# A fixed order of work in layers 1 to 3, dense and listed tiles mixed, and smaller table rows in layer 0, in a four-layer graph attention kernel

## The chip, the cores and the metric

The kernel runs on one core of one Trainium2 chip. The metric is the device time of one execution in microseconds; lower is better. Before the change it is 4248.78 us, the median of three runs (4247.72, 4248.78 and 4255.99).

## The reference: what is computed

There are 4096 nodes with 256 features and a 0/1 adjacency matrix of 4096 x 4096 whose density falls from the first node to the last, so the first rows have many neighbours and most rows few. Four attention layers follow one another, each as `x = layernorm(x + layer(x, adj))`:

```python
# layer 0, 8 heads: a neighbour j of i weighs
#   exp(leaky_relu(e_l[i] + e_r[j], 0.2) + gate * sum_f |c[i,f] - c[j,f]| * Wc[h,f])
# layer 1, one head: weight exp(s_src[i] + s_dst[j])
# layer 2, 4 heads: exp(leaky_relu(s_row[i] + s_col[j], 0.2)); elu(out) + x @ Wr + br, then a layernorm of its own
# layer 3, one head, three times: h = x @ W0, then h = elu(softmax(mask(leaky_relu(f1 + f2.T, 0.01))) @ (h @ W))
```

Each weight is masked by the adjacency and divided by its row's sum. A row without any neighbour takes the mean over all nodes instead, which the kernel carries as `cs`.

## The kernel before, in words

**Lists.** For each block of columns of the result (128 destination rows in layer 0, 256 in the later layers, called a pair, `PW`) the kernel finds the nodes with at least one edge into it. From the adjacency it makes bytes on ScalarE (`ab`, L669), counts edges per node on TensorE (`flags`, L676), ranks them (`places`) and builds each list by comparing ranks with a counter on VectorE (`here`, L715, four instructions a list) and 32 small matmuls on TensorE (`list_p`, L729). A list has a fixed number of tiles of 128 nodes: `SLOT_TILES` for layer 0 (373 in all) and `PAIR_TILES` for the pairs (251 without the first). For a listed pair the mask is gathered too, one tile at a time (`pair_m`, L742, and `pair_mb`, L746), and stored in DRAM.

**Layer 0** first projects x (class `Projection`, `rows`), scales the result and writes it into `table0`, one row of 368 numbers per node: 264 weighted features, 8 factors, and the node's 6 curvature numbers repeated 16 times (96). Then `rows0` walks over the 373 tiles, in blocks of 3 or 4 tiles (107 blocks). A tile's table rows `g` and adjacency cells `m` are gathered by indirect DMAs on GpSimd (L419, L421). Per block TensorE transposes the curvature part of each `g` (`cj_p`, L431), ScalarE copies it and makes 8 differences `d` (L438). Per tile TensorE computes the scores `s` (2 x L453, 16 x L457), ScalarE takes `e = exp(s)` (L459), VectorE multiplies in the row factors (8 x L475), and TensorE adds the products to `acc` (16 x L481), two tiles later. This loop stands under `tc.manual_schedule`: TensorE, VectorE and ScalarE run their instructions in the order in which the program writes them. In each tile's round the program writes: `edges` (the mask `ne` of the next tile, L445), `pair_terms` (scores and `e`), `weights`, the `add` of two tiles before, one third of the next block's `differences` (`parts`), one step of a row end (`end`), and `lane(n + 1)`. The lane takes 1.5 steps a tile from one generator, `all_groups`, in which flags and lists of the later groups follow one another, and one job (`step`): a piece of a mask.

**Layers 1 to 3.** `layer1`, `layer2` and `layer3` loop over pairs (`plan_of`: two dense pairs, then listed pairs with the other dense pairs between), and within a pair over its tiles. A dense pair has 32 tiles, all nodes, whose rows lie in SBUF; a listed pair's rows are gathered from a table in DRAM (`Nodes.rows`, L908). Per tile VectorE (in layer 1 `nc.any`, ScalarE or VectorE) makes the weights `w` (L983, L1048, L1121), and TensorE multiplies (L991; L1050 for the sums and L1053 for the denominators; L1123). After a pair's last tile the program writes its whole row end: `quotients`, the residual and layernorm, and the projection for the next layer (`project_rows`; `Projection.steps`, with `xT` L182, `ph` L186, `V` L189, `f2` L190, and for layers 2 and 3 a separate product `pf` L197 for the second score vector, which goes through DRAM). These layers have no order written out by hand: the compiler's own scheduler places the instructions of each engine by priority and readiness in its model. `DENSE` gives the number of dense pairs: 6 in layer 1, one in layer 2, 3 in each pass of layer 3.

Of the kernel before, what the change touches and what calls it, by code (L numbers as in the profile page):

```python
# [49 lines left out]
F32 = mybir.dt.float32  # L50
# [19 lines left out]
DENSE = {1: 6, 2: 1, 3: 3}  # L70


@with_exitstack
def gnn_stack(ctx: ExitStack, tc: tile.TileContext, a: dict, out: bass.AP):
# [36 lines left out]


    class Projection:
# [6 lines left out]

        def __init__(self, name, nh, scores, nf, w, wt, V=None, f1=None, bias=None, pre=None, extra=None,
                     done=None):
            self.name, self.nh, self.nf, self.V, self.f1, self.bias, self.extra = name, nh, nf, V, f1, bias, extra
            self.w, self.wt, self.scores, self.pre, self.done = w, wt, scores, pre, done
            self.f2 = carry.tile([P, NT, nh], F32, name=f"{name}_f2", tag="f2")
            self.xs = carry.tile([P, 2, NT], F32, name=f"{name}_xs", tag="xs")
            self.cs = carry.tile([P, nh, C // nh + 1], F32, name=f"{name}_cs", tag="cs")

        def prepare(self, st, ps):

            self.ps = ps
            nh, nf = self.nh, self.nf
            wp = st.enter_context(tc.tile_pool(name=f"{self.name}_w", bufs=1))
            self.xp = st.enter_context(tc.tile_pool(name=f"{self.name}_x", bufs=2))
            wx = wp.tile([P, 2, C + nf], F32, name="wx")
            nc.gpsimd.dma_start(wx[:, :, 0:C], self.w.rearrange("(k p) o -> p k o", p=P))
            wt = wp.tile([P, 2, C], F32, name="wt")
            nc.gpsimd.dma_start(wt, self.wt.rearrange("(k p) o -> p k o", p=P))
            amat = wp.tile([P, 2, nf], F32, name="amat")
            nc.vector.memset(amat, 0.0)  # L140
            for kt, p0, n, col, vec in self.scores:
                nc.gpsimd.dma_start(amat[p0:p0 + n, kt, col:col + 1], vec)
            for mt in range(2):
                pw = ps([P, nf], "pw")
                for kt in range(2):
                    nc.tensor.matmul(pw, wt[:, kt, mt * P:(mt + 1) * P], amat[:, kt, :], start=kt == 0, stop=kt == 1)
                nc.vector.tensor_copy(wx[:, mt, C:], pw)
            if self.pre is not None:
                pre = wp.tile([P, 2, C], F32, name="pre")
                nc.gpsimd.dma_start(pre, self.pre.rearrange("(k p) o -> p k o", p=P))  # L150
                both = wp.tile([P, 2, C + nf], F32, name="both")
                for mt in range(2):
                    pw = ps([P, C + nf], "pw")
                    for kt in range(2):
                        nc.tensor.matmul(pw, pre[:, kt, mt * P:(mt + 1) * P], wx[:, kt, :], start=kt == 0, stop=kt == 1)
                    nc.vector.tensor_copy(both[:, mt, :], pw)
                wx = both
            self.wx = wx
            if self.bias is not None:
                self.bx = wp.tile([P, C + nh], F32, name="bx")  # L160
                nc.gpsimd.dma_start(self.bx[:, 0:C], self.bias.partition_broadcast(P))
                bcol = wp.tile([P, 2, 1], F32, name="bcol")
                nc.gpsimd.dma_start(bcol, self.bias.rearrange("(k p o) -> p k o", p=P, o=1))
                wide = wp.tile([P, 2, P], F32, name="bwide")
                nc.vector.tensor_copy(wide, bcol.to_broadcast([P, 2, P]))
                pb = ps([P, nf], "pb")
                for kt in range(2):
                    nc.tensor.matmul(pb, wide[:, kt, :], amat[:, kt, :], start=kt == 0, stop=kt == 1)
                nc.vector.tensor_copy(self.bx[:, C:], pb[:, 0:nh])
            if self.extra is not None:  # L170
                self.wr = wp.tile([P, 2, C], F32, name="wr")
                nc.gpsimd.dma_start(self.wr, self.extra[0].rearrange("(k p) o -> p k o", p=P))

        def steps(self, T, x):

            nh, ps = self.nh, self.ps
# [7 lines left out]
            ph = ps([P, C + nh], "ph")  # L184
# [1055 lines left out]
```

## Time and profile before

| what | value |
|---|---|
| median of three runs | 4248.78 us |
| the profiled execution | 4770.22 us, its span 4768.5 us |
| start, until the first score matmul of layer 0 | 0 to 243 us |
| loop of layer 0 | 243 to 2165 us |
| change from layer 0 to layer 1 | 2165 to 2195 us |
| layer 1 | 2195 to 2640 us |
| layer 2 | 2640 to 3440 us |
| layer 3, three passes | 3440 to 4768 us |
| TensorE, VectorE, ScalarE, GpSimd busy | 81%, 59%, 38%, 51% of the span |
| mean granted TensorE clock | 0.877 |

The borders of the stages are read from the first and last start of each line's instructions. The profiled execution is 12.3% longer than the median of the plain runs, so its stages show shares rather than absolute times. A matmul's recorded duration is longer than the step from one matmul to the next, because matmuls overlap: work on TensorE is read from starts in the timeline. A row of the groups view gives the line, engine, operation, tiles, count, the union of busy time and the mean of one, then the engine's idle time just before these instructions and what ended it.

### The profile page before, as it was taken

To read this page: it belongs to the slowest core of one execution; us is meant where nothing else is said; L and a number is where in the kernel's file an instruction comes from. 1 tells how busy PE (TensorE), PEld (TensorE's weight loads), DVE (VectorE), ACT (ScalarE), POOL (GpSimd) and SP (SyncE) were. 2 spreads that over 40 slices of the span, in tenths; PEclk is the share of its full clock that TensorE was granted. 3 is DMA by queue.
4 is the path that set the end of the run, shared out by engine and by line. 5 is a ranking of instruction groups with operands and counts; after the bars stand their busy time and mean duration, and the time that the engine had idled before them with its cause. 6 is when DMAs were issued, how large, how long until landed. Compare 5 with 4: busy or idle time off the path is not lost. (4 is left out here: it accounts for less than half of the span.)

```text
span 4768.5 us, 79015 instructions
## 1 busy us (share of the span) xinstructions
PE 3878.5 (81%) x27461; PEld 2801.1 (59%) x27461; DVE 2814.2 (59%) x8948; ACT 1810.2 (38%) x3869; POOL 2453.5 (51%) x2123
## 2 busy tenths in 40 slices
PE   5478889788888888896678799999877878786877
PEld 3267777677767676685566233333365756565665
DVE  5257687675757576564345667778754444444555
ACT  2265666565656565573445011222211110111123
POOL 3067565666666666531342256665336434643455
PEclk7788889898888898896889799999988989897988
DMA  4344655444454443434343323333233342333344
GB/s 131 97 154 116 189 164 174 135 133 132 128 132 125 121 125 90 105 78 127 106 114 104 93 69 83 93 95 103 85 102 103 87 117 84 104 88 114 107 121 119
DMA packets 389766, 541.97 MB, mean 114 GB/s; under 512 B 123400, under 2 KB 292334, under 8 KB 389342
## 3 DMA queue, kind: packets, MB, share of 16 engines
q1 hardware_dynamic: 290400, 270.70, 20.8%
q0 software_dynamic: 98960, 266.15, 19.8%
q8 instruction: 220, 3.60, 0.3%
q14 instruction: 186, 1.52, 0.1%
HBM read 469.34 MB, written 67.26 MB: 113 GB/s over the span
## 5 line engine op out<-in xcount | busy, mean ns | idle before, releaser
L908 POOL DMA_INDIRECT g<-table,pair_idx x1010 | 1191.7, 1180 | 1240.4 <-DVE rden L313 277.3
L475 DVE SCALAR_TENSOR_TENSOR e<-R,g,e 128x128 f32<-128x128 f32 x2984 | 816.4, 344 | 554.5 <-ACT e L459 419.4
L457 PEld LDWEIGHTS s<-kw,d 97*128 97x128 f32 x5968 | 895.0, 213 | 150.9 <-issue 97.5
L457 PE MATMUL s<-kw,d 97*128 97x128 f32 x5968 | 911.2, 298 | 42.1 <-issue 32.2
L419 POOL DMA_INDIRECT g<-table,idx x373 | 457.0, 1225 | 469.0 <-PE acc L481 136.1
L1123 PE MATMUL acc<-g,w 128*128 128x257 f32 x2448 | 617.4, 407 | 78.2 <-issue 39.9
L421 POOL DMA_INDIRECT m<-in_adjT,idx x373 | 473.8, 1270 | 269.2 <-ACT ne L445 93.5
L459 ACT ACTIVATE e<-s 128x1024 f32<-128x1024 f32 x373 | 380.0, 1019 | 599.2 <-PE s L457 312.8
L1123 PEld LDWEIGHTS acc<-g,w 128*128 128x128 f32 x2448 | 479.7, 202 | 188.9 <-issue 69.1
L1121 DVE SCALAR_TENSOR_TENSOR w<-R,g,mask 128x256 f32<-128x256 f32 x612 | 289.9, 481 | 382.1 <-PE acc L1123 242.9
L438 ACT ACTIVATE d<-cj,ci 97x384 f32<-97x384 f32 (+1 forms) x856 | 510.2, 658 | 3.5
L481 PE MATMUL acc<-e,g 128*33 128x128 f32 x5968 | 460.4, 293 | 51.6 <-issue 39.5
L1048 DVE SCALAR_TENSOR_TENSOR w<-R,g,mask 128x256 f32<-128x256 f32 x1004 | 417.1, 468 | 7.6 <-DMA g<-table,pair_idx 5.9
L481 PEld LDWEIGHTS acc<-e,g 128*33 128x33 f32 x5968 | 329.3, 118 | 128.8 <-issue 62.8
L1050 PE MATMUL num<-w,g 128*64 128x256 f32 x2008 | 384.2, 402 | 13.3 <-issue 7.3
L453 PE MATMUL s<-ne,far 128*128 128x512 bf16 x746 | 310.5, 416 | 58.1 <-ACT ne L445 36.2
L300 ACT ACTIVATE elu_neg<-y 128x256 f32<-128x256 f32 x128 | 52.9, 413 | 801.9 <-DVE y L315 631.0
L742 POOL DMA_INDIRECT pair_m<-in_adjT,cell x251 | 293.9, 1171 | 122.9 <-issue 49.9
L1123 PE MATMUL acc<-V,w 128*128 128x257 f32 x1152 | 280.6, 404 | 63.8 <-DVE w L1121 42.0
L186 PE MATMUL ph<-wx,xT 128*128 128x257 f32 (+2 forms) x640 | 218.0, 471 | 101.8 <-ACT xT L182 67.3
L1123 PEld LDWEIGHTS acc<-V,w 128*128 128x128 f32 x1152 | 229.3, 202 | 109.3 <-DVE w L1121 45.7
L1053 PE MATMUL den<-w,g 128*1 128x256 f32 x2008 | 271.3, 381 | 6.8 <-issue 6.8
(267 smaller groups left out, 4409.0 us busy)
## 6 DMA issues: line engine op xcount, KB each, us to landing
ai<-in_adj SPq DMA_DIRECT2D x128, 512.0 KB
mask<-listed_d SPq DMA_DIRECT2D x228, 128.0 KB
at<-in_adjT SPq DMA_DIRECT2D x96, 256.0 KB
R<-r_d SPq DMA_DIRECT2D x32, 512.0 KB
mask<-mask_d SPq DMA_DIRECT2D x128, 128.0 KB
g<-table,pair_idx POOLq DMA_INDIRECT x1010
table<-V SPq DMA_DIRECT2D x12, 1032.0 KB
s<-y SPq DMA_DIRECT2D x96, 128.0 KB
```

What stands on the lines that cost most here:

```text
L419: nc.gpsimd.indirect_dma_start(g[:, :], None, table0[:, :], bass.IndirectOffsetOnAxis(ap=idx[:, 0, k:k + 1], axis=0))
L421: nc.gpsimd.indirect_dma_start(m[:, :], None, cells, bass.IndirectOffsetOnAxis(ap=idx[:, 1, k:k + 1], axis=0))
L438: nc.scalar.activation(self.d[:, g, 0:n], cj[:, 0:n], AF.Relu, bias=ci[:, k:k + 1])
L453: nc.tensor.matmul(s[:, q:q + 4], far, by_group[:, q:q + 4].unsqueeze(2).to_broadcast([P, 4, H0, L]), start=True, stop=False)
L457: nc.tensor.matmul(s[:, g], self.d[:, g, k * P:(k + 1) * P], kw_flat, start=False, stop=g == q + 3)
L459: nc.scalar.activation(e.rearrange("p h (g l) -> p g h l", l=L), s, AF.Exp)
L475: nc.vector.scalar_tensor_tensor(e[:, h, :], self.R[:, h, :], g[:, VW + h:VW + h + 1], e[:, h, :], ALU.max, ALU.mult)
L481: nc.tensor.matmul(self.acc[o:o + D0 + 1, h // 2, :], g[:, h * (D0 + 1):(h + 1) * (D0 + 1)], e[:, h, :], start=False, stop=last and h >= H ...
L908: nc.gpsimd.indirect_dma_start(g[:, :], None, self.table[:, :], bass.IndirectOffsetOnAxis(ap=pair_idx[:, at:at + 1], axis=0))
L1048: nc.vector.scalar_tensor_tensor(w[:, h], R[:, h], g[:, VW2 + h:VW2 + h + 1], m, ALU.max, ALU.mult)
L1050: nc.tensor.matmul(num[h % 2 * D2:(h % 2 + 1) * D2, h // 2, :], g[:, h * (D2 + 1):h * (D2 + 1) + D2], w[:, h], start=False, stop=k == A - ...
L1123: nc.tensor.matmul(t, w[:, it * P:(it + 1) * P], g[:, 0:C + 1], start=k == 0, stop=k == A - 1)
```

## The change

Six things change together.

- **Layers 1 to 3 get a written order.** A new function `attend` walks over a sequence of tiles under `manual_schedule`: weights of this tile, products of the tile `lag` before (in layer 2 two tiles at a time, all their sums and then all their denominators), and `rate` steps of the row ends.
- **Dense tiles are mixed with listed ones.** `sequence` replaces `plan_of`: the first `LEAD` dense tiles stand alone, the others are spread evenly among the listed tiles.
- **Row ends become generators** (`one`, `elu_steps`, `norm_steps`, `project`), so that a row end is spread over many tiles. Residual rows are loaded earlier, results are written from ScalarE's DMA queue, quotients are reshaped (`inverse`), and in layer 2 some of the work moves to ScalarE (y, four instructions) and GpSimd (`xb + beta`).
- **The projection takes both score vectors in one product** (`nf` more columns in `ph`; `pf` and its way through DRAM go), and `row_factors` works on the transposed form. Parameter loads move from GpSimd's to SyncE's queue and to the start of a layer. The features' scaling in layers 2 and 3 moves from VectorE to ScalarE, the table writes of layers 1 to 3 from SyncE's to GpSimd's queue.
- **Lists of layer 0 run in two lanes**, flags in one and lists in the other, at most one step of each per tile; a list's matmuls come two steps after its last comparison. Before the loop only the first group's flags and its first list are made, after the projection instead of ahead of it.
- **Smaller table rows:** `table0` holds the 6 curvature numbers once (278 numbers a row), and VectorE repeats them 16 times in a new copy `c` per tile, ahead of the transpose. Buffers: `got` 16 to 13, `e` 4 to 3 in layer 0; work buffers 4 to 6 in the later layers.

```diff
+LEAD = {1: 80, 2: 32, 3: 44}
...
-    TW = VW + H0 + KF
+    TW = VW + H0 + CF
...
-            got = st.enter_context(tc.tile_pool(name="l0_got", bufs=16))
+            got = st.enter_context(tc.tile_pool(name="l0_got", bufs=13))
...
                     pt = ps([KF, JR * P], "cj_p")
                     for k, g in enumerate(self.rows):
-                        nc.tensor.transpose(pt[:, k * P:(k + 1) * P], g[:, VW + H0:], ident)
+                        c = three.tile([P, L, CF], F32, name="c", bufs=5)
+                        nc.vector.tensor_copy(c, g[:, VW + H0:].unsqueeze(1).to_broadcast([P, L, CF]))
+                        nc.tensor.transpose(pt[:, k * P:(k + 1) * P], c.rearrange("p l f -> p (l f)"), ident)
...
+            lanes = [[all_flags(), 0.0], [list_steps(entries[1:]), 0.0]]
...
             def lane(n):
-                while done[0] < 1.5 * n:
-                    done[0] += 1
-                    next(groups, None)
-                step()
+                for k, rate in enumerate((0.8 if n < 40 else 0.65, 1.0 if n < 24 else 0.62)):
+                    lanes[k][1] += rate
+                    if lanes[k][1] >= 1.0:
+                        lanes[k][1] -= 1.0
+                        next(lanes[k][0], None)
+                job()
...
-            ph = ps([P, C + nh], "ph")
+            ph = ps([P, C + nf], "ph")
...
-            if self.f1 is not None:
-                pf = ps([nh, P], "pf")
-                for kt in range(2):
-                    nc.tensor.matmul(pf, self.wx[:, kt, C + nh:], xT[:, kt, :], start=kt == 0, stop=kt == 1)
-                self.f1(T, pf)
...
+    def sequence(dense, listed, lead):
+        first = [(q, k, NT, False) for q in dense for k in range(NT)]
+        later = [(q, k, PAIR_TILES[q], True) for q in listed for k in range(PAIR_TILES[q])]
+        order, rest = first[:lead], first[lead:]
+        given = 0
+        for n, t in enumerate(later):
+            order.append(t)
+            while given * len(later) < len(rest) * (n + 1) and given < len(rest):
+                order.append(rest[given])
+                given += 1
+        return order + rest[given:]
+
+    def attend(seq, opened, weights, products, ends, rate=1.0, batch=1, lag=2):
+        states, ready, ended, due = {}, [], [], 0.0
+        end = ends(ended)
+        with tc.manual_schedule(engines={mybir.EngineType.PE, mybir.EngineType.DVE, mybir.EngineType.Activation}):
+            def multiply(n):
+                some, ready[:] = ready[:n], ready[n:]
+                products(some)
+                ended.extend(state for state, _, _, last in some if last)
+            for q, k, A, listed in seq:
+                if k == 0:
+                    states[q] = opened(q, A, listed)
+                ready.append((states[q], k, weights(states[q], k), k == A - 1))
+                if len(ready) == lag + batch:
+                    multiply(batch)
+                due += rate
+                while due >= 1.0:
+                    due -= 1.0
+                    next(end, None)
+            while ready:
+                multiply(min(batch, len(ready)))
+            drain(end)
...
+            attend(seq, opened, weights, products, lambda ended: ends_of(ended, NP, nxt, ps, one), rate=1.6, batch=2)
```

## The prediction

> **What bounds the kernel now.** I read the page first. No engine is full and the chain that ended last covers only the end of the run, so the stages have to be taken one by one.
>
> ```profile
> PE 3878.5 (81%) x27461; PEld 2801.1 (59%) x27461; DVE 2814.2 (59%) x8948; ACT 1810.2 (38%) x3869; POOL 2453.5 (51%) x2123
> PEclk7788889898888898896889799999988989897988
> ```
>
> Next the windows view: stretch and its length, then busy time (and instructions) of TensorE, its weight loads, VectorE, ScalarE and GpSimd, granted clock, DMA share, GB/s.
>
> ```profile
> 0.00:243.00 243.00, 118.10 (x712) 74.75 (x713) 89.45 (x244) 60.20 (x200) 53.05 (x116) 0.72 0.39 117
> 243.00:2165.00 1922.00, 1630.63 (x15633) 1391.84 (x15632) 1271.81 (x4264) 1154.51 (x2005) 1192.91 (x972) 0.89 0.47 130
> 2195.00:2640.00 445.00, 327.19 (x1805) 265.60 (x1806) 196.21 (x729) 201.99 (x620) 143.91 (x147) 0.80 0.40 115
> 2640.00:3440.00 800.00, 750.43 (x4980) 250.27 (x4978) 593.12 (x1743) 154.52 (x375) 441.26 (x264) 0.96 0.34 88
> 3440.00:4768.00 1328.00, 1038.33 (x4294) 809.53 (x4294) 653.90 (x1927) 229.73 (x643) 618.31 (x619) 0.87 0.38 105
> ```
>
> In layer 1 VectorE is busy 44%, ScalarE 45% and GpSimd 32%; in layer 3 VectorE 49%. TensorE's busy time overlaps itself, so I took its real step from the timeline of layer 3:
>
> ```profile
> 3599.72 4.50 PE L1123 MATMUL acc<-g,w 128*128 128x257 f32 x20
> ```
>
> (4.50 - 0.38)/19 = 0.217 us; 3600 of them need 781 us of the 1328. So layers 1 to 3 mostly wait. Layer 2's waits and groups show for what:
>
> ```profile
> DVE p_f L190 <- ACT V L189: 130.5, 30, 13.4
> L1048 DVE SCALAR_TENSOR_TENSOR w<-R,g,mask 128x256 f32<-128x256 f32 x1004 | 417.1, 468 | 7.6 <-DMA g<-table,pair_idx 5.9 <-PE den L1053 1.1 <-remote 0.5
> 2780.62 21.06 POOL L908 DMA_INDIRECT g<-table,pair_idx  x1 [2.81 <-PE den L1053]
> ```
>
> VectorE stands 4.4 us in each of 30 projections of a row end, with the next weights behind it. The last line matters later. In layer 0's loop (groups of TensorE, then its timeline):
>
> ```profile
> L729 PE MATMUL list_p<-rhs,here 128*128 128x18 bf16 (+13 forms) x1344 | 47.0, 174 | 77.0 <-DVE here L715 45.6 <-issue 16.1 <-DVE rhs L724 8.3
> L676 PE MATMUL flags<-ones_b,ab 128*128 128x1 bf16 x896 | 32.0, 164 | 47.2 <-ACT ab L669 27.8 <-issue 9.6 <-ACT d L438 9.3
> ...
> 1207.87 0.60 PE L676 MATMUL flags<-ones_b,ab 128*128 128x1 bf16 x18
> 1211.53 0.35 PE L676 MATMUL flags<-ones_b,ab 128*128 128x1 bf16 x8 [1.80 <-ACT d L438]
> 1211.74 0.38 PE L453 MATMUL s<-ne,far 128*128 128x512 bf16 x1
> ```
>
> Flags hold TensorE 3.9 us, and the next scores queue behind them. The loop's 1922 us are 5.15 us a tile; nothing in it is full.
>
> [...] granted clock 0.72 in the start, 0.96 in layer 2. [...] a gather, usually 0.95 us, took 21.06 us during an unbroken run of L1048. [...]
>
> **The change part by part,** against the span of 4768.5 us.
>
> *Start, 243 us.* Before, the first group's flags and five lists go ahead of most of the projection, whose rows then come at 2.45 us each (starts of L190). Without `pf` (four products at 0.11 us) a row takes about 2.0 us: 32 give 64 us after some 33 us of setup. Flags and one list (here 4 x 1.2, the rest about 5 us) add 15 us beyond that, shifts, table and its writes 28 us, first gathers 20 us (the trace has 35 from the first gather to the first score). Sum 160, saved 83; bounds 140 and 200.
>
> *Layer 0's loop.* Gains: a flag step no longer shares a tile with its last edge step, and a list's matmuls come later. The two rows' idle time is 124 us; with 28 flag groups at up to 3.9 us, and 42 lists at 2.3 (47.8 us in 21 waits for L715), at most about 206. I take a tile at 4.3 us instead of 4.9 where nothing else intervenes: VectorE 2.19 (L475) + 1.2 (L715) + 0.3 (pair_mb) + 0.5. Smaller gathers gain nothing: DMA is busy 47%. Loss: the new copy `c`. It isn't in the trace; the smallest VectorE copies are 0.15 and a 24x128 one 0.21, so 0.17 us, or 0.6 us a block. The price is its place. It stands on VectorE behind this tile's weights, and the transposes stand on TensorE ahead of the next scores. So once a block the chain is serial: scores 2.3 (1204.56 to 1206.87), e 1.0, weights 2.2, copies 0.6, transposes 0.5, waits 0.4: 7.0 us until the next scores can start. Before, these transposes needed only the gather. 107 x 7.0 + 266 x 4.3 = 1893; half clock adds what it adds now to L457 (mean 298 against median 275, 8% of the TensorE links): about 55. I take 1950 against 1922: +28. Bounds: 1800 if slack hides half of what the copy's place costs (1660 if all, rival 2), 2175 if ScalarE too is late at these tiles (then 9.1 us). Buffers 13 and 3 cost nothing: three blocks are 12 tiles, and e(n) needs the products of n-3, which stand ahead of its scores on TensorE anyway; without this cover a gather would wait one round, 5 us a block.
>
> *Change to layer 1, 30 us*: left.
>
> *Layer 1.* TensorE: 1356 products, 0.12 us each from starts, 163; row ends (ph, pr, transposes) 58 without `pf`; 221 in all, at clock 0.87 254. GpSimd: 147 gathers at 1.25 (0.95 and 0.30 idle) 184, beginning about 48 us in, after 8 MB of loads and table writes at 180 GB/s (stretches between stages move 154 to 196): 232. ScalarE and VectorE need some 160 each. The 80 leading dense tiles cover the table. With a tail of 20: 275, saved 170. Bounds 245 and 320.
>
> *Layer 2.* VectorE: 283 tiles x 4 x 0.396 (55 in 21.84 us) = 448; row ends 32 x 3.1 (seven wide ones at 0.33-0.37 and small ones) = 99. Start 30, last row end 25. Waits of rows on TensorE and ScalarE shrink from 4.4 to perhaps 2.5 us: 80. Grouped sums and denominators take TensorE about 1.4 us a tile, below VectorE's 1.6. Sum 682, and 8 for gathers that come late: 690, saved 110. The 128 small ScalarE instructions for the features (about 0.25 each by the 128x32 rows, 32 us) lie beside 50 us of weights of the first pair. Bounds 620 and 760.
>
> *Layer 3.* TensorE a pass: 1200 x 0.217 = 260, projection 35, and with fewer pauses at layer 2's clock, 0.95, 310. Between passes 38, other stalls 10: 358, twice. The last pass has no projection: GpSimd 204 x 1.25 = 255 from 35 us on, then its tail: 340. Sum 1056, say 1060, saved 268. Without the listed rows' cover by 44 dense tiles (38 us) each pass would begin with the table's 22 us of writes. Bounds 1000 and 1180. The added ScalarE DMA issues (about 0.35 each as on SyncE, 32 a layer) lie beside an engine busy 17% there.
>
> Sum: 160 + 1950 + 30 + 275 + 690 + 1060 = 4165, or 603 less than 4768. I scale by the shares: 4165 / 4768.5 x 4248.78 = **3711 us**. Bounds put together by squares: -180 and +271, 3551 to 3953.
>
> **The rivals.**
> 1. *Layer 0 gives a good part back.* The serial tile takes 9.1 us, since ScalarE comes late and half clock follows each pause: 107 x 2.1 = +225, 3912 us. For it: three engines in fixed order and a pause of 2.7 us a block[...]. Against: the loop's last tiles, without lists, take 3.9 us, so there is slack.
> 2. *More is gained*: the copy's place is hidden and all 373 tiles take 4.3 plus the clock's 55: 1660, 3452 us in all. Against: TensorE has no other work to put there, as order is fixed.
> 3. *Slower: gathers starve in layer 2.* If a gather runs only while VectorE is idle, a listed tile is serial: weights 1.58, row ends 0.3, gather and landing 3.7 (207.88 to 211.57 in the start): 5.6 x 251 + 116 = 1522, 832 more than forecast, 4452 us. It decides from 4.7 us a listed tile (my 603 are gone then). For it: the 21.06 us. Against: in the first pair's unbroken 63 us of weights 15 of 16 gathers took about a microsecond[...].
> 4. *The order isn't what costs*: layers 1 to 3 keep their 2573 us, the rest holds: 4713, 4199 us.
>
> **How the numbers follow.** Forecast 60%, rival 1 18%, rival 2 8%, rival 3 10%, rival 4 4%. The predicted time is 3711; its own range 3551 to 3953. With rivals 1 and 2 taken in the range is 3450 to 3980, which leaves out rivals 3 and 4 and some edge. Less than 0.2% is what a measurement here can't tell from no change: faster 0.89, same 0.01, slower 0.10 (rival 4 falls nearly all on the faster side).
>
> **What the profile after would show.** Right: the first score near 160 us; waits of flags and list matmuls gone, but TensorE's cj_p waiting on VectorE's `c` about 107 times, 2 to 3 us each; layer 1 near 275 us; VectorE over 80% busy in layer 2, its wait for V small; layer 3's passes near 350 us with TensorE's products nearly gapless. The prediction is wrong if gathers of tens of microseconds spread in layer 2, if VectorE's wait for a row end moves to another instruction of it, if the wait for `c` is much longer than 3 us, or if plain runs are not shortened in the profile's proportion.

## The result and the profile after

The kernel after takes 4298.82 us (median of four runs, 4281.02 to 4304.84) against 4248.25 us for the kernel before beside it: ratio 1.0112, 95% interval 1.0075 to 1.0150. It is slower by 1.1%, where 3711 us were forecast; the range (3450 to 3980) missed it and the sign was wrong.

The profiled execution's span is 4303.1 us, in line with the plain times. From the page of the kernel after, the busy time of each engine and the granted clock in 40 slices:

```profile
PE 3480.2 (81%) x26823; PEld 2779.7 (65%) x26823; DVE 2781.4 (65%) x8850; ACT 1919.3 (45%) x4242; POOL 2375.5 (55%) x2125
PEclk9688888888988888989979889999898998998998
```

TensorE has 638 fewer instructions (the `pf` products are gone) and VectorE does nearly the same work; no engine is full now either. The windows view of the kernel after, by stage (length, then busy time and instructions of TensorE, weight loads, VectorE, ScalarE, GpSimd, then granted clock, DMA share, GB/s):

```profile
0.00:159.00 159.00, 87.34 (x457) 65.12 (x457) 49.87 (x156) 57.12 (x212) 29.17 (x87) 0.83 0.57 165
159.00:2156.00 1997.00, 1619.61 (x15757) 1418.50 (x15756) 1347.23 (x4681) 1164.00 (x2004) 1158.40 (x973) 0.87 0.40 117
2185.00:2556.00 371.00, 292.33 (x1693) 258.24 (x1693) 203.20 (x724) 181.62 (x592) 151.31 (x157) 0.85 0.49 140
2556.00:3309.00 753.00, 572.81 (x4869) 272.58 (x4869) 603.95 (x1636) 221.23 (x633) 415.36 (x286) 0.90 0.32 92
3309.00:4303.00 994.00, 895.24 (x4014) 756.98 (x4014) 568.19 (x1614) 285.21 (x776) 621.25 (x623) 0.95 0.49 138
```

The start is what was forecast (159 against 160). The loop of layer 0 takes 1997 us, not 1950. Layers 1 and 2 take 371 and 753 instead of 275 and 690, layer 3 takes 994 instead of 1060 (these borders are not quite the prediction's, see the table below). The waits for `here` and for flags, 124 us in the loop before, are gone as foretold. From TensorE's groups of the kernel after:

```profile
L720 PE MATMUL list_p<-rhs,here 128*128 128x18 bf16 (+16 forms) x1504 | 48.7, 180 | 0.4 <-ACT cj L417 0.2
L664 PE MATMUL flags<-ones_b,ab 128*128 128x1 bf16 x1024 | 32.9, 164 | 4.7 <-ACT ab L657 4.5
```

In their place, from the page's groups:

```profile
L415 PE MATMUL cj_p<-ident,c 128*96 128x128 f32 x373 | 87.3, 367 | 392.3 <-DVE c L414 392.3
```

TensorE now stands 392 us ahead of these transposes, all of it for the new copy `c`. One such wait, from the timeline of the kernel after (start, duration, engine, line; in brackets the idle time before and who ended it), TensorE first, then ScalarE, then VectorE:

```profile
1316.44 1.05 PE L441 MATMUL s<-kw,d 97*128 97x128 f32 x8
1317.42 1.07 PE L465 MATMUL acc<-e,g 128*33 128x128 f32 x16
1321.60 0.55 PE L415 MATMUL cj_p<-ident,c 128*96 128x128 f32 x3 [3.10 <-DVE c L414]
1321.99 0.38 PE L437 MATMUL s<-ne,far 128*128 128x512 bf16 x1
1322.20 1.65 PE L441 MATMUL s<-kw,d 97*128 97x128 f32 x8
1323.64 0.63 PE L437 MATMUL s<-ne,far 128*128 128x512 bf16 x1
1324.07 1.92 PE L441 MATMUL s<-kw,d 97*128 97x128 f32 x8
...
1317.58 1.02 ACT L443 ACTIVATE e<-s 128x1024 f32<-128x1024 f32 x1 [2.46 <-issue]
1322.19 0.48 ACT L417 COPY cj<-cj_p 96x384 f32<-96x384 f32 x1 [3.58 <-PE cj_p L415]
1322.70 1.12 ACT L422 ACTIVATE d<-cj,ci 97x384 f32<-97x384 f32 x2
1326.02 1.03 ACT L443 ACTIVATE e<-s 128x1024 f32<-128x1024 f32 x1 [1.05 <-PE s L441]
...
1319.23 2.19 DVE L459 SCALAR_TENSOR_TENSOR e<-R,g,e 128x128 f32<-128x128 f32 x8
1321.34 0.45 DVE L414 COPY c<-g 128x96 f32<-128x96 f32 x3
1327.08 0.35 DVE L459 SCALAR_TENSOR_TENSOR e<-R,g,e 128x128 f32<-128x128 f32 x1 [5.10 <-ACT e L443]
```

From one `e` (1317.58) to the next (1326.02) this tile takes 8.44 us, one engine after another: `e` 1.02, 0.63 until VectorE has finished list work, weights 2.19, copies and transposes to 1321.99, then scores for 4.0 us instead of 2.3. Eight scores take 1.65 and 1.92 us here and 1.05 before the pause. The windows view shows why, with a granted clock of 0.50 in this stretch (1.00 from 1317.4 to 1318.5 and from 1326 to 1330):

```profile
1322.50:1325.90 3.40, 3.40 (x16) 3.04 (x15) 0.00 (x0) 2.44 (x5) 2.73 (x3) 0.50 0.33 99
```

The two `d` of the timeline belong to the next block; these scores don't wait for them. Over the whole kernel TensorE waits 5.4 us, in 19 waits, for a `d`.

The same happens in most blocks. In 106 of the 107 TensorE pauses for more than 2 us at these transposes (median 2.98), and in 88 the 18 score products behind them take more than 3.3 us (median of all 3.9, of those at a granted clock of 1.00 2.4). Over these 18 products the granted clock is 0.59 in the median of all blocks, and 0.50 to 0.70 in the 88 with slow scores. Of 53 blocks with a pause of 2 to 3 us, 40 have slow scores; of 53 with a longer one, 47. In the kernel before, slow scores follow these transposes in 21 blocks (first trace) or 14 (before_third, see below).

### The profile page after: what moved, and what is told of

It is laid out like the page before. It is cut to its first block, busy times and chain, and to the rows that moved or that the text cites. A ratio compares the mean times of both kernels' runs of the same rounds, so it can differ in the third digit from the quotient of the medians.

```text
span 4303.1 us, 78043 instructions
## 1 busy us (share of the span) xinstructions
PE 3480.2 (81%) x26823; PEld 2779.7 (65%) x26823; DVE 2781.4 (65%) x8850; ACT 1919.3 (45%) x4242; POOL 2375.5 (55%) x2125
## 5 line engine op out<-in xcount | busy, mean ns | idle before, releaser
L954 POOL DMA_INDIRECT g<-table,pair_idx x1010 | 1140.1, 1129 | 601.8 <-PE den L1157 101.2
L441 PEld LDWEIGHTS s<-kw,d 97*128 97x128 f32 x5968 | 925.3, 221 | 69.3 <-issue 19.3
L1243 PE MATMUL acc<-g,w 128*128 128x257 f32 x2448 | 581.5, 386 | 31.8 <-DVE w L1237 31.6
L465 PE MATMUL acc<-e,g 128*33 128x128 f32 x5968 | 414.8, 283 | 0.0
L415 PE MATMUL cj_p<-ident,c 128*96 128x128 f32 x373 | 87.3, 367 | 392.3 <-DVE c L414 392.3
L1153 PE MATMUL num<-w,g 128*64 128x256 f32 x2008 | 318.9, 422 | 54.1 <-DVE w L1144 51.1
L733 POOL DMA_INDIRECT pair_m<-in_adjT,cell x251 | 266.7, 1063 | 147.8 <-DVE pair_mb L737 77.6
L415 PEld LDWEIGHTS cj_p<-ident,c 128*96 128x96 f32 x373 | 51.4, 152 | 421.4 <-DVE c L414 356.1
L1153 PEld LDWEIGHTS num<-w,g 128*64 128x64 f32 x2008 | 158.3, 148 | 197.0 <-DVE w L1144 131.2
L1253 ACT ACTIVATE y<-acc,inverse 128x256 f32<-128x256 f32 x96 | 45.7, 476 | 519.9 <-DVE inverse L307 472.9
```

The source lines that it names most:

```text
L441: nc.tensor.matmul(s[:, g], self.d[:, g, k * P:(k + 1) * P], kw_flat, start=False, stop=g == q + 3)
L465: nc.tensor.matmul(self.acc[o:o + D0 + 1, h // 2, :], g[:, h * (D0 + 1):(h + 1) * (D0 + 1)], e[:, h, :], start=False, stop=last and h >= H ...
L954: nc.gpsimd.indirect_dma_start(g[:, :], None, self.table[:, :], bass.IndirectOffsetOnAxis(ap=pair_idx[:, at:at + 1], axis=0))
L1153: nc.tensor.matmul(num[h % 2 * D2:(h % 2 + 1) * D2, h // 2, :], g[:, h * (D2 + 1):h * (D2 + 1) + D2], w[:, h], start=False, stop=last and ...
L1243: nc.tensor.matmul(t, w[:, it * P:(it + 1) * P], g[:, 0:C + 1], start=k == 0, stop=last)
```

## The experiments

The base of a diff is the kernel after unless said otherwise. Stage times are read from the first and last start of each stage's instructions, as in the prediction but for two borders named below the table.

### Two unchanged kernels, three times: which chip is it?

The plain runs of before (4248 us) and its profiled execution (span 4768.5 us) differ by 12%. Both kernels were therefore run again as they are.

> The kernel before, unchanged, profiled once more. Theory A (the one profiled execution of 4768.5 us was not typical: some stage of it ran slower than in plain runs): this time the span is 4240 to 4300 us, and the stages that shrink against the first trace are the ones whose share misled the scaling. Rival B (recording slows this program always, because of how its instructions wait): the span is again 4700 to 4800 us while the plain time stays at 4250, and the stages are as in the first trace.

> The kernel before, unchanged, profiled beside the kernel after on one chip. Theory A2 (chips differ: the traces of 4768 and 4740 us come from slower chips than the plain times of 4248 us, and the forecast scaled across two chips): its span is near 4250 us where the kernel after takes about 4300, or near 4740 where the kernel after takes more than 4303. Rival B2 (the kernel before has two speeds on any chip): its span and its plain times differ by some 500 us on the same chip.

> The kernel after, unchanged. Theory A2: beside a kernel before of about 4740 us it takes 4550 to 4800 us (ratio 0.96 to 1.01), since a slower chip slows both; its loop of layer 0 stays near 2000 us, because it is held by a chain of engine work and not by what differs between the chips. Beside a kernel before of 4250 us it takes 4300. Rival B2: 4303 us on every chip.

> The kernel after once more. On a chip that takes some 4230 us for the kernel before: 1.012 again. On one that takes some 4740 us, where the profile named waits on nothing of the program in layers 1 to 3: the serial tile of layer 0 costs there what it costs elsewhere (about 309 us over the run with early copies, which took 4373 us there), so 4680 us and 0.989, faster than before. If the loss is the same on every chip: 1.012 there too.

Measured: before_again 4739.91 us, with a span of 4740.4 us, and 4733.13 us for the kernel before beside it (1.0023, 0.9995 to 1.0052). before_third 4229.7 us, span 4226.5 us, 4233.81 us beside it (0.9993, 0.9981 to 1.0006). So it is not the profiling that lengthens an execution: there are two conditions, one in which the kernel before takes some 4230 us ("fast chip" here and in the expectations) and one in which it takes some 4740 us ("slow chip"). By their times, the plain runs of before and after belong to the first, the trace of before to the second. Chip 9 was fast, chips 5, 7 and 15 were slow, chip 7 twice within 54 minutes; of the first runs the chip isn't on record. No chip was seen both ways, so that the chip itself makes the difference, and not something that lasted on it for a while, is not shown.

The kernel after was then measured on both: after_again 4287.3 us, 1.0121 (1.0092 to 1.0151) on a fast chip; after_third 4640.74 us against 4753.85 us, 0.9747 (0.9700 to 0.9793) on a slow one. The sign depends on the chip. I had expected 0.989 there. By stages, in us:

| stage | forecast (slow) | before, slow | after, slow | before, fast | after, fast |
|---|---|---|---|---|---|
| start | 160 | 239 | 176 | 236 | 164 |
| layer 0 | 1950 | 1919 | 2076 | 1791 | 1982 |
| change | 30 | 30 | 30 | 33 | 27 |
| layer 1 | 275 | 471 | 426 | 372 | 367 |
| layer 2 | 690 | 793 | 762 | 764 | 751 |
| layer 3 | 1060 | 1288 | 1170 | 1030 | 995 |

The borders of layers 2 and 3 are here the first weights of each. The prediction's lay some 34 us earlier (2640 against 2674.0, 3440 against 3473.5 in its trace), so its 275 and 1060 stand for about 309 and 1026 in this table.

What differs between the chips can be seen in the waits view. It writes "remote" where it finds no recorded instruction or transfer whose end fits the event that ended a wait. From the profile of before that the prediction was read from (engine, what waited and its line: us in total, times, longest):

```profile
DVE w L1121 <- remote: 129.2, 51, 5.8
ACT e L459 <- remote: 106.9, 23, 11.4
ACT xT L182 <- remote: 79.6, 18, 19.2
POOL g L908 <- remote: 56.5, 40, 2.8
```

The trace of before_third has no such line, nor has that of the kernel after, nor any other taken on a fast chip; all taken on slow chips have them (the view's lines sum to 527 us over all engines in before_again, 347 in after_third). Followed back, they are waits for TensorE: in the slow traces 2194 of 2195 such waits end with a step of the one semaphore that TensorE's matmuls raise, only later than the end recorded for any matmul allows. The longest in the profile of before, from its timeline:

```profile
2258.22 0.69 PE L180 MATMUL xT_p<-ident,y 128*128 128x128 f32 x2 [2.08 <-issue]
2278.62 2.10 PE L186 MATMUL ph<-wx,xT 128*128 128x260 f32 x4 [18.42 <-ACT xT L182]
2278.20 0.28 ACT L182 ACTIVATE xT<-xT_p 128x128 f32<-128x128 f32 x1 [19.25 <-remote]
```

Two transposes are recorded as done at 2258.91, and ScalarE, which reads them, starts at 2278.20, 0.02 us after TensorE's semaphore moved. So on a slow chip TensorE, or its report that a result is there, stopped for up to 19 us in the middle of work. Why it stops is not in the traces.

Layer 3 shows what that does. The windows view of before_again (slow), then of before_third and of after_again (both fast):

```profile
3600.00:3650.00 50.00, 38.13 (x155) 29.66 (x153) 22.00 (x61) 5.95 (x22) 32.95 (x34) 0.88 0.41 110
```

```profile
3245.00:3295.00 50.00, 50.00 (x238) 41.59 (x237) 30.01 (x82) 7.26 (x28) 26.79 (x27) 1.00 0.34 98
```

```profile
3340.00:3390.00 50.00, 50.00 (x237) 43.71 (x236) 27.69 (x73) 8.76 (x32) 38.12 (x40) 1.00 0.49 133
```

On the slow chip TensorE gets 155 instructions done in 50 us at clock 0.88. On the fast one the old order did 238 at full clock, and the written order does 237. There was nothing left to take out of these stretches, which make up some 40% of the layer there, though the trace from the slow chip seemed full of gaps.

Layer 1 is the same case with a loss. Windows of before_third, then of after_again:

```profile
2240.00:2260.00 20.00, 18.94 (x132) 16.35 (x131) 13.86 (x53) 15.01 (x48) 10.63 (x11) 1.00 0.47 132
2300.00:2320.00 20.00, 19.58 (x134) 16.87 (x134) 17.82 (x67) 16.49 (x54) 15.43 (x16) 1.00 0.63 178
```

```profile
2340.00:2360.00 20.00, 17.24 (x98) 14.91 (x98) 11.16 (x39) 9.45 (x31) 11.67 (x13) 0.83 0.53 155
2380.00:2400.00 20.00, 17.54 (x116) 16.50 (x115) 13.16 (x46) 11.31 (x39) 12.36 (x13) 0.91 0.57 161
```

From 2120 to 2360 us the old order does 111 to 135 matmuls in 20 us (105 in the stretch before); from 2260 to 2500 the written one does 75 to 116, at a granted clock of 0.83 to 0.91 in all but one stretch, where the old order had 1.00 in all but one. It starts the layer sooner and loses that again.

### Layer 0: the place of the copy

The copies of block b+1 are moved ahead of the scores of the first tile of block b, so that they stand on VectorE behind the weights of an earlier tile; the work is the same.

```diff
+                def copies(self):
+                    self.wide = []
+                    for g in self.rows:
+                        c = three.tile([P, L, CF], F32, name="c", bufs=5)
+                        nc.vector.tensor_copy(c, g[:, VW + H0:].unsqueeze(1).to_broadcast([P, L, CF]))
+                        self.wide.append(c)
...
-                    for k, g in enumerate(self.rows):
-                        c = three.tile([P, L, CF], F32, name="c", bufs=5)
-                        nc.vector.tensor_copy(c, g[:, VW + H0:].unsqueeze(1).to_broadcast([P, L, CF]))
+                    for k, c in enumerate(self.wide):
...
+                        if b + 1 in blocks:
+                            blocks[b + 1].copies()
```

> The kernel after with the copies c of the next block written ahead of the tile's scores and weights instead of behind them; the number of copies is the same. Theory 1 (the copy's place on VectorE is what layer 0 loses): the wait of TensorE for c, 392 us in the kernel after, falls below 40 us, the first tile of a block falls from 9.0 to about 5 us, the loop of layer 0 from 1999 to about 1600 us, the whole to 3850 to 3950 us, ratio 0.91 to before. Rival 2 (the loop is held by ScalarE and VectorE work anyway, the wait for c only shows where the slack is): the wait moves to e or ne, the loop stays above 1900 us and the whole above 4200 us.

> The copies c ahead of the weights, beside the kernel after. Theory 1: 150 to 400 us below the kernel after on the same chip, all of it in the loop of layer 0, since the layers behind are the same code. Rival 2 (the wait for c was slack): within 60 us of it.

Measured: 4373.28 us, 0.9245 (0.9211 to 0.9280) on a slow chip; 3978.57 us, 0.9393 (0.9363 to 0.9422) on a fast one, where the kernel after beside it took 4287.3. So 309 us on the fast chip hang on the place of one copy. The loop falls from 1982 to 1674 us; from the starts of `e`, a block's first tile falls from 9.0 to 6.2 us, and the others stay at 3.8. It is less than I expected: TensorE still waits 184 us for `c` (from 394), not under 40, and the first tile is not near 5.

The second way takes the copies out: rows of 368 numbers again, read by the transposes directly, as before (two `got` buffers fewer, for space).

```diff
-    TW = VW + H0 + CF
+    TW = VW + H0 + KF
...
-                        c = three.tile([P, L, CF], F32, name="c", bufs=5)
-                        nc.vector.tensor_copy(c, g[:, VW + H0:].unsqueeze(1).to_broadcast([P, L, CF]))
-                        nc.tensor.transpose(pt[:, k * P:(k + 1) * P], c.rearrange("p l f -> p (l f)"), ident)
+                        nc.tensor.transpose(pt[:, k * P:(k + 1) * P], g[:, VW + H0:], ident)
```

> The kernel after with the smaller table rows undone: 368 numbers a row, no copies c, the transposes read the gathered rows. For room in memory the gathered rows have 11 buffers instead of 13. Theory 1: within 60 us of the kernel with early copies, the wait of TensorE for c gone. Rival 3 (the copies themselves and not their place cost, through VectorE's time): clearly below the kernel with early copies, by 60 us or more. Eleven buffers may add a wait of some gathers, up to 5 us a block.

> Table rows of 368 numbers and no copies, layers 1 to 3 as in the kernel after; it stands here as the base for the three runs beside it. Theory now (on an undisturbed chip layers 1 to 3 of the kernel before were already close to what their fullest engine allows): 0.93 of the kernel before on a fast chip, 0.91 to 0.93 on one that takes some 4730 us for it; layers 1 to 3 near 361, 755 and 994 us on the fast one. The prediction's theory (the written order is worth hundreds of us in layers 1 to 3) has no other number for it, since it is the same in both.

Measured: 3950.25 us, 0.9337 (0.9306 to 0.9369) on a fast chip; 4363.03 us, 0.9169 (0.9141 to 0.9198) on a slow one. On the fast chip that is 28 us below the early copies, within the 60 that I expected. The loop takes 1639 us on the fast chip. The idle time before the instructions on tile `cj_p`, by what ended it, in the kernel after and then in wide_rows:

```profile
  DVE c L414: 748.4, 201
  PE cj_p L415: 418.3, 106
```

```profile
  DMA g<-table,idx: 309.0, 103
  PE cj_p L413: 171.6, 93
```

(The first line of each counts TensorE and its weight loads, the second is ScalarE's copy.) Without the copy the transposes wait for the gather, and much less. The larger rows cost nothing that can be seen: the other tiles stay at 3.8 us. On the fast chip layers 1 to 3 take 363, 754 and 995 us with early copies and 361, 755 and 994 with wide rows, as in the kernel after, so the whole difference is layer 0's. Against the kernel before on that chip, wide_rows saves 72 us in the start, 152 in the loop and 59 behind it. What saves the 152 was not taken apart; the lists in two lanes, whose waits are gone, are the likely part.

### Layers 1 to 3: what the parts of the change are worth

These start from wide_again; all were run on slow chips. First the written order is taken away from layers 1 to 3, with the sequence of tiles and the row ends in steps kept:

```diff
     def attend(seq, opened, weights, products, ends, rate=1.0, batch=1, lag=2):
-        with tc.manual_schedule(engines={mybir.EngineType.PE, mybir.EngineType.DVE, mybir.EngineType.Activation}):
+        with ExitStack():
```

> The base, with the written order of TensorE, VectorE and ScalarE in layers 1 to 3 left to the scheduler, as it was before; sequence of tiles, steps and everything else stay. Prediction's theory: the order removes the waits, so without it layers 1 to 3 take 300 to 550 us longer, 1.08 to 1.14 of the base. Rival 4 (the order isn't what costs): within 60 us of the base, 0.985 to 1.015 of it, with TensorE's products in layer 1 denser than in the base (130 or more in 20 us at full clock against 100 to 115) and more time lost at the ends of the layers.

> Rows of 368 numbers without copies, and the order of the engines in layers 1 to 3 left to the scheduler. If the written order costs on any chip because it ties TensorE to the row ends: 0.915 to 0.925 of the kernel before on a fast chip (the written order had 0.934), with layer 1 some 30 us or more shorter than 391 us from the end of layer 0 to the start of layer 2. If it costs only where the chip stalls by itself: 0.930 to 0.936 on a fast chip. On a slow chip 0.90 again.

> Rows of 368 numbers without copies, all order in layers 1 to 3 left to the scheduler. On a chip that takes some 4230 us for the kernel before, where the written order had 0.934: 0.915 to 0.925 if the written order costs on any chip, 0.930 to 0.936 if only where the chip stalls by itself. On one that takes some 4750 us: 0.90 again.

Measured: 4287.81, 4299.17 and 4291.44 us, 0.9013 (0.8985 to 0.9041), 0.9039 (0.8987 to 0.9090) and 0.9014 (0.8988 to 0.9040), all on slow chips. Against wide_again beside the first (4363.03) the run is 75 us **shorter**: the written order costs time. Layer 1, windows of wide_again, then of wide_free:

```profile
1990.00:2418.00 428.00, 312.87 (x1693) 272.56 (x1693) 203.37 (x725) 180.74 (x591) 150.38 (x157) 0.81 0.43 121
```

```profile
2002.00:2365.00 363.00, 282.53 (x1706) 253.15 (x1706) 189.37 (x725) 181.07 (x592) 151.93 (x157) 0.87 0.50 143
```

Nearly the same instructions take 65 us less, at a granted clock of 0.87 instead of 0.81. Layer 3 gains 39 us (1163 to 1124) and layer 2 loses 22 (765 to 787). That suggests keeping the written order in layer 2 alone (the only one with `batch` over 1):

```diff
-        with ExitStack():
+        with tc.manual_schedule(engines={mybir.EngineType.PE, mybir.EngineType.DVE, mybir.EngineType.Activation}) if batch > 1 else ExitStack():
```

> As the run beside it, but with layer 2 in written order (it took 765 us so against 788 us free). If the stage times add up: 15 to 25 us shorter than the run beside it, 0.994 to 0.997 of it. If free order in layer 2 only moved time to and from its borders: within 0.2% of it.

> Layer 2 in written order, layers 1 and 3 left to the scheduler. 15 to 25 us shorter than the run beside it on either kind of chip (it was 27 us there), 0.994 to 0.997 of it, if layer 2 alone gains from its written order.

Measured: 4272.32 us beside 4299.17, and 4278.61 beside 4291.44: 0.994 and 0.997 of free order, and 0.8980 (0.8939 to 0.9020) and 0.8990 (0.8952 to 0.9029) of the kernel before. That the gain is layer 2's is not shown: against the free order beside it, layer 2 is 13 us shorter in the first pair of traces (768 against 781) and 2 in the second (775 against 777). It is the best version found on a slow chip, by little; none without written order fell on a fast one, so there the best measured is wide rows at 0.9337, and whether the written order costs there too stays open.

Next, free order with the sequence of the kernel before:

```diff
     def sequence(dense, listed, lead):
-        first = [(q, k, NT, False) for q in dense for k in range(NT)]
-        later = [(q, k, PAIR_TILES[q], True) for q in listed for k in range(PAIR_TILES[q])]
...
+        first, later = list(dense[:2]), list(dense[2:])
+        n = -(-len(listed) // (len(later) + 1))
+        order = [(q, k, NT, False) for q in first for k in range(NT)]
+        for m in range(len(later) + 1):
+            order += [(q, k, PAIR_TILES[q], True) for q in listed[m * n:(m + 1) * n] for k in range(PAIR_TILES[q])]
+            order += [(q, k, NT, False) for q in later[m:m + 1] for k in range(NT)]
+        return order
```

> As the run with all order left to the scheduler, and with the sequence of the kernel before: two dense pairs, then list pairs in a row with the other dense pairs whole between them. If mixing dense among list tiles is what helps (gathers every 1.25 us are slower than the products of two tiles): 30 to 90 us longer than the run with mixed tiles, above all in layer 3, where TensorE then shows gaps behind gathers. If the sequence makes no difference: within 15 us of it.

Measured: 4420.62 us, 0.9278 (0.9226 to 0.9330), beside 4299.17, so 121 us longer, most of it in layer 3 (1230 against 1131 us). Mixing dense among listed tiles helps. With the stage sums of layers 1 to 3 on slow chips (change included): before 2582, old sequence in free order 2437, mixed sequence in free order 2302, written order 2385. So what is neither order nor sequence (row ends in steps, no `pf`, earlier loads, other queues; not taken apart) is worth about 145 us, the mixing 135, and the written order takes back 83. These sums are over slow chips alone; on the fast chip the kernel after gains 59 us in all here.

Two attempts to find what the written order waits for, each from wide_again: one step between a projection's products and their readers, so that a tile's weights stand between; and products four tiles behind the weights in layers 1 and 3.

```diff
             if self.bias is None:
+                yield
                 nc.scalar.copy(self.V(T), ph_h)
```

> The base, with one step put between a projection's products and what ScalarE and VectorE read from them in layers 1 to 3, so that a tile's weights stand between. If the waits that the fixed order itself leaves on VectorE (71 us in layer 2, 62 us in layer 1 at the line that copies the features) are on the path: those waits fall to under 15 us in each layer and the run is 60 to 120 us shorter, 0.97 to 0.985 of the base. If TensorE and VectorE only pass the time on (the next wait in the row end takes it): within 20 us of the base.

```diff
-            attend(seq, opened, weights, products, lambda ended: ends_of(ended, NP, nxt, ps, one))
+            attend(seq, opened, weights, products, lambda ended: ends_of(ended, NP, nxt, ps, one), lag=4)
```

> The base, with the products of layers 1 and 3 four tiles behind their weights, where they were two behind. If layer 1 is held by short stalls of TensorE behind a row end (19 gaps of 1.5 us or more, 50 us, and a clock of 0.83 to 0.91 after them): those gaps shrink to under 20 us, the clock rises to 0.95 or more between the first and last row end, and layer 1 takes 320 to 340 us instead of 361; layer 3's passes stay within 10 us. If TensorE's own products are the limit of layer 1 as they stand: within 10 us in all.

Measured: 4358.63 us, 0.9167 (0.9135 to 0.9199), and 4365.02 us, 0.9172 (0.9135 to 0.9209), beside 4363.03: no difference. But neither edit removed what it aimed at. In layer 1 of wide_later VectorE's wait for ScalarE's copy `V` of a projection fell only from 70 to 45 us while the one for `Vg` rose from 40 to 56, and in wide_lag layer 1 took 431 us instead of 428, at a clock of 0.80 instead of 0.81. So these runs don't tell which wait counts. The view that separates wide_again from wide_free in layer 1 is VectorE's and ScalarE's waits; first wide_again, then wide_free:

```profile
ACT rs L321 <- DVE mv L291: 59.5, 13, 7.1
DVE Vg L1031 <- ACT Vg L1030: 40.3, 42, 3.2
```

```profile
DVE Vg L1031 <- ACT Vg L1030: 11.2, 9, 4.5
```

ScalarE's wait for the moments of a row end (59.5 us) is no longer among its longest in free order, and VectorE's wait for ScalarE's piece of a gathered tile falls from 40.3 to 11.2 us. In a written order ScalarE stands at `rs` with the next tiles' casts behind it, and VectorE then waits for those. That this is the whole 65 us was not tested.

## Why the prediction was wrong

The forecast was 538 us less than before; the kernel after takes 50 us more. Three steps failed: the worth of the written order, the size of layer 0's serial tile, and the scaling.

**"So layers 1 to 3 mostly wait"**, and the written order takes the waits away: this is the largest. Its 548 us (170, 110 and 268) are 194 on the slow chip that the trace came from (2582 to 2388) and 59 on the fast one. The order itself has no part in them: taken away from wide_again on a slow chip, it makes the kernel 75 us shorter. By the sums above the gain is the mixing and what comes with the row ends in steps. Part of the idle time that I counted as waits for row ends was the late results of TensorE, which the change leaves in place: ScalarE's `xT` alone stood 79.6 us for them in the trace of before and 65.1 in after_third. So the sum fails already on its own chip: 4165 us against 4640, with 16 us of the miss in the start, 126 in layer 0 and 333 in layers 1 to 3.

**"I scale by the shares"** turned 4165 us into 3711, on the belief that the profiled execution shows the stages of the plain runs 12% longer. It shows another condition. On the fast chip the kernel before is not shorter in proportion: layer 0 is 7% shorter, layers 1 and 3 about 20%, layer 2 4%. The idle time to be won in layers 1 and 3 was largely absent there, so 113 us of gain on a slow chip (the two medians beside each other) are 53 us of loss on a fast one. The profile gave two warnings that I passed over: a span 12% above the plain median, and waits on "remote". The closing condition of the prediction ("if plain runs are not shortened in the profile's proportion") is what happened.

**Start**: right, 83 us forecast, 73 to 77 measured on the fast chip, 63 on the slow one.

**Layer 0**: the mechanism was right, a serial chain once a block, and the size of one term too small. A block's first tile was put at 7.0 us and takes 9.0, the others at 4.3 and take 3.85: 107 x 9.0 + 266 x 3.85 = 1987, against 1982 and 1997 measured. What the 7.0 left out is on the timeline above: 0.6 us of list work ahead of the weights, and scores of 4.0 instead of 2.3 us, with a granted clock of 0.50 for 3.4 us of them. My separate 55 us for half clock spread over the loop what falls on these tiles. That 1950 came within 50 us is luck: some 214 us too little on the first tiles, some 120 too much on the others. On the fast chip before, the two were 5.4 and 4.5 us. Against before, the loop loses 191 us on the fast chip and 157 on the slow one, where I had +28; the two runs without the late copy show that this alone turns a gain of 6 to 7% into a loss of 1.2%.

**Layer 1**: 275 forecast (309 on the table's borders), 371 measured. The step of 0.12 us was right: in the kernel after, these products start 0.121 us apart in the median. What was put at nothing are TensorE's own waits. From its first to its last product, by the windows view, and the longest of its waits in that stretch:

```profile
2185.00:2515.00 330.00, 275.46 (x1642) 247.18 (x1643) 188.44 (x663) 164.47 (x528) 149.90 (x155) 0.87 0.50 145
PE acc L1063 <- DVE w L1052: 19.3, 16, 3.1
```

At the clock that I assumed, 0.87, it is busy 275 us, where I had 254, and idle 55, waiting for weights, for copies of gathered tiles and for row ends. Another 41 us pass until the first weights of layer 2; I had 20 for this tail and 30 for the start of layer 2.

**Layer 2**: 690 forecast, 753 measured. The weights took 476 us (not 448), from VectorE's groups of the kernel after:

```profile
L1144 DVE SCALAR_TENSOR_TENSOR w<-R,g,mask 128x256 f32<-128x256 f32 x1004 | 425.2, 494 | 6.9 <-issue 4.2 <-DMA g<-table,pair_idx 2.8
L1144 DVE SCALAR_TENSOR_TENSOR w<-R,V,mask 128x256 f32<-128x256 f32 x127 | 50.5, 481 | 0.0
```

Row ends took 128 us (604 busy less 476), not 99, and VectorE stood 149 us, not 143. VectorE was 80% busy as foretold; but on the fast chip it had already been busy 596 of 764 us before the change, so there was little to win.

**Layer 3**: 1060 forecast; 995 on the fast chip and 1170 on the slow one. In the full stretches of the fast chip products are nearly gapless, as foretold, but before they were too.

**The rivals.** Rival 1 was right about the serial tile (9.1 us; 9.0 measured) and, in 88 of 107 blocks, about slow scores after the pause (granted clock 0.50 to 0.70), but not that ScalarE comes late (5.4 us of waits for `d` in all); its loop of 2175 us didn't come, since the other tiles are shorter, and its 3912 us take layers 1 to 3 and the scaling over from the forecast. Rival 2 is excluded by the 9.0 us. Rival 3, slow gathers in layer 2, came in part and cost next to nothing; that a gather runs only while VectorE is idle was my estimate from one of 21.06 us. Over the 251 gathers there, from the kernel after,

```profile
L954 POOL DMA_INDIRECT g<-table,pair_idx x251: 944/965/25553, 2587.3 to 3228.7; - x126
```

(least, median and longest, ns). Thirteen of them, about one for each listed pair, take more than 3 us, 129 us together, while VectorE is busy 73 to 99% of the time; in the trace that I read before there were 16. During 177 of the other 238, none over 2.5 us, VectorE is busy 73% or more too, so its work alone doesn't explain the long ones, and what held them is not shown. VectorE waited only 2.8 us for gathers (layer 2's first line above), so they did not decide. Rival 4, that order is not what costs, had 4% and was nearest: layers 1 to 3 gain 59 us on the fast chip. Its 4199 us failed on layer 0. None of the rivals had the case that came: layers 1 to 3 give little and layer 0 loses more than the start gains.

## What to carry to other kernels

The profile whose span was far from the plain times (4768.5 us against 4248) was a profile of other conditions: compare the spans first, follow waits without a named cause to what they wait for, and forecast the change in microseconds for the conditions in which it will be timed, not in shares of the other. A repeating chain that passes through all engines once a block should be followed to its end, with the clock after its pause (here 0.50 to 0.70 over the scores of 88 blocks): a copy that costs 0.45 us a block took 2.8 us a block only by its place. And a change of many parts can hide its best ones: on the fast chip the place of one copy cost 309 us, more than all the other parts together brought (255 us, with early copies), and on slow chips the written order took back 83 us of the 280 that the rest of the change brought in layers 1 to 3.

## What the runs showed of the hardware

- The same kernel takes some 4230 us on one chip and 4733 to 4763 on three others, with spans that agree with the plain times on each. In the traces of those three and in the first trace of the kernel before, and only there, TensorE's semaphore comes late again and again, by up to 19 us after the recorded end of its matmuls (217 such waits of other engines in before_again, none in before_third), and the engines that wait for TensorE stood 527 us in all in before_again. Why is open. The stages suffer unequally: before the change layer 3 took 1288 instead of 1030 us, layer 2 793 instead of 764. So the change made the kernel faster by 2.5% on a slow chip and slower by 1.2% on the fast one.
- In the kernel after, where TensorE pauses once in a block of 17 to 21 us, the 18 score products behind the pause took more than 3.3 us in 40 of 53 blocks with a pause of 2 to 3 us and in 47 of 53 with a longer one, at a granted clock of 0.50 to 0.70. In the first trace of the kernel before they took as long in 19 of the 105 blocks without a pause of more than 2 us. In the block shown of the kernel after the granted clock was 0.50 for 3.4 us, from 0.9 us after the pause on: eight score matmuls took up to 1.92 us there and 1.05 before the pause.
- About one gather for each listed pair of layer 2 took 3 to 26 us, with VectorE busy 73 to 99% of the time, as it was during 177 of the 238 shorter ones; the median gather took 0.965 us.
